# Layer 1's output projection as seven block products on two PSUM tiles

## The chip, the core and the metric

The kernel runs on one core of a Trainium2 chip. The metric is the device time of one execution in microseconds (us). The engines of a core work through their own instruction queues, each in order, and wait for each other by semaphores: TensorE (PE in the profile, its weight loads PEld), VectorE (DVE), ScalarE (ACT), GpSimd (POOL), and SyncE (SP), which here issues most of the DMAs.

## The reference

Two attention layers with group norm in front and a residual around each, on x of 128 rows x 256 positions x 256 channels, in float32. Layer 0 is row attention with a pair bias from z and a gate. Layer 1, where the change is, is banded attention:

```python
qkv = x2 @ w_in.T + b_in                 # x2 = group norm of x, (128, 256, 256)
q, k, v = heads of qkv                   # 4 heads of 64
scores = einsum('bhid,bhjd->bhij', q, k) / sqrt(64)
scores = where(|i - j| <= 16, scores, -inf)
out = einsum('bhij,bhjd->bhid', softmax(scores), v)
y = out @ w_out.T + b_out
x = x + y
```

The last product, `out @ w_out.T`, is the output projection.

## The kernel before

Layer 1 handles the 128 rows in 64 pairs (`NP`); class `Pair1` holds one pair, and its two rows are numbered `r` = 0 and 1. Channels lie on the partitions in two blocks (`KC` = 2) of 128; positions are cut in two blocks (`NB` = 2) of 128.

The order of all instructions is written out by hand: under `tc.manual_schedule()` every engine gets its instructions in the order in which the Python code makes them. The loop `for p in range(NP - 1)` (line 2169) has five pairs in hand: `was` (p - 1) is finished, `now` (p) has its scores and its first row applied, `nxt` (p + 1) has q, k and v computed, `nn` (p + 2) is normalised, and `n3` (p + 3) is loaded and transposed. One iteration has, in order:

- `now.scores(0)`, `now.scores(1)`: scores of both rows on PE (L2013), exponentials on ACT (L2022), the band's mask multiplied in by POOL (L2024).
- `was.apply(1)`: exponentials times v, and the sums of the exponentials, for row 1 (L2038, L2046). Even and odd key blocks go to two accumulators each. ACT copies the odd one (`copy_sums` L2057, `copy_odd` L2060), DVE adds the even one (`join_sums` L2063, `join_odd` L2066), `invert` takes the reciprocal (L2069), and `weigh` multiplies the two into `oT` (L2074), from SBUF to SBUF.
- Between these stand `nxt.product(n, i)` and `nxt.join(n, i)` for q (n = 0) and k (n = 1), and later for v (n = 2). q, k and v are made of 2 x 2 blocks each; seven block products in place of eight suffice, with sums of weight blocks (`wst`, made once by `mix_weights`) and of input blocks (`dT`, made by `differences` on POOL, L1922 to L1925). Products 1, 6, 7, 4 run up one accumulator x: after each, ACT copies what stands there (to `u`, or as an output block), before the next product is added on it. Products 2, 5, 3 use a second accumulator y, and after each a `join` on DVE adds y and a copy in `u` to give an output block. q and k use tiles of 256 columns (L1960), v uses two halves of 128 (L1956). x and y are whole PSUM tiles of tags `s0` and `s1`, shared with the scores; q and v use `s0`, k uses `s1`.
- `was.out_row(0)`, and further down `was.out_block(1, 0)` and `was.out_block(1, 1)`: the output projection. A row takes two blocks of positions, and a block takes two products of 256 columns (L2092). `keep_row` adds the residual `xt` on DVE (L2100), and after row 1 SP writes the pair out (L2108).
- `nn.centre(k)`: normalisation on ACT (L1909). `nn.add_bias()`: the residual plus the output bias on POOL (L1915). `n3.turn()`: transposition on DVE (L1904). `some_checks`: comparisons on DVE from a queue of checks, two an iteration until the queue is empty, more in the last eight pairs.

In this order the two blocks of `was.out_row(0)` stand between products 7 and 4 of q and k, `was.join_odd(1)` stands after the joins 5, and `nn.centre(1)`, `nn.differences()`, `nn.add_bias()` and `n3.turn()` are at the end of the iteration.

[...]Four are the tags `s0` and `s1`, two hold `o_eo`, the even and odd outputs of `apply`. The last two are one tile `su_y` of shape `[P, 2, 2, I]`: its first half of each bank (`su_eo`) takes the sums of even and odd blocks, its second halves together take the projection of a row (`self.y`).

SP issues in the order of the code too: the loads of a pair (`xs` in four DMAs and `xt`) when `Pair1` is made, at the start of an iteration, then the sums of `weigh` (L2079), then the output.

Of the kernel before, what the change touches and what calls it, by code (L numbers as in the profile page):

```python
# [773 lines left out]
def fast_kernel(  # L774
# [134 lines left out]
    def rows(ap, s0, n):  # L909
        return ap[s0 : s0 + n].rearrange("s (b p) c -> p (s b) c", p=P)  # L910
# [914 lines left out]
    with tc.tile_pool(name="l1", bufs=2) as sb, tc.tile_pool(  # L1825
# [10 lines left out]
        dev = lrs[0][:, :G]  # L1836
        each = head.rearrange("p n d -> p (n d)").rearrange("p (n c) -> p n c", n=2)
        wst = sb.tile([P, 4, 3, P], F32, name="wst", bufs=1)

        def norm1():  # L1840

# [20 lines left out]
        def mix_weights():  # L1862

            a = [[w_in[:, k].rearrange("p (n m c) -> p m n c", n=3, m=KC)[:, m] for k in range(KC)]
                 for m in range(KC)]
            s1, s2, s3, s4 = (wst[:, n] for n in range(4))
            nc.gpsimd.tensor_tensor(s1, a[1][0], a[1][1], ALU.add)
            nc.gpsimd.tensor_tensor(s2, s1, a[0][0], ALU.subtract)
            nc.gpsimd.tensor_tensor(s3, a[0][0], a[1][0], ALU.subtract)
            nc.gpsimd.tensor_tensor(s4, a[0][1], s2, ALU.subtract)  # L1870


        o_eo = [ps_o.tile([P, 2, I], F32, name=f"ps_o1_{n}", tag=f"o{n}") for n in range(2)]
        su_y = ps_o.tile([P, 2, 2, I], F32, name="ps_su_y1", tag="su")
        su_eo = [su_y[:, n, 0] for n in range(2)]
        for n in range(2):
            nc.vector.memset(o_eo[n], 0.0)
        nc.vector.memset(su_y, 0.0)

        class Pair1:  # L1880

# [54 lines left out]
            def product(self, n, i):  # L1936

                if len(self.ps) == n:
                    self.ps.append([mm1("ps_qk", n % 2) for _ in range(2)])
                    self.u.append(sm.tile([P, 3, I], F32, name="u1", tag=f"u{n}", bufs=2))  # L1940
                x, y = (ps[:, :I] for ps in self.ps[n])
                w = lambda m, k: w_in[:, k, n * C + m * P : n * C + (m + 1) * P]
                b = lambda k, r: self.xgT[:, k, r * I : (r + 1) * I]
                to, lhs, rhs, start = {
                    1: (x, w(0, 0), b(0, 0), True),
                    2: (y, w(0, 1), b(1, 0), True),
                    6: (x, wst[:, 1, n], self.dT[:, 1], False),
                    5: (y, wst[:, 0, n], self.dT[:, 0], True),
                    7: (x, wst[:, 2, n], self.dT[:, 2], False),
                    4: (x, w(1, 1), self.dT[:, 3], False),  # L1950
                    3: (y, wst[:, 3, n], b(1, 1), False),
                }[i]
                if n == 2:
                    for b in range(NB):
                        at = slice(b * P, (b + 1) * P)
                        nc.tensor.matmul(  # L1956
                            to[:, at], rhs[:, at], lhs, start=start and b == 0, stop=True, skip_group_check=True
                        )
                else:
                    nc.tensor.matmul(to, lhs, rhs, start=start, stop=True, skip_group_check=True)  # L1960
                u = self.u[n]
                if i in (2, 5, 3):
                    return
                at = (1, 6, 7, 4).index(i)
                to = self.to[n](1, 0) if i == 4 else u[:, at]
                if n == 2:
                    nc.scalar.copy(to, x.rearrange("p (b c) -> p b c", b=NB) if i == 4 else x)
                else:
                    nc.scalar.activation(to, x, AF.Identity, bias=bin_c[:, n * KC + (at > 1) : n * KC + (at > 1) + 1])  # L1969
# [59 lines left out]
            def apply(self, r):  # L2029


                e = self.es[r]
                gap = q0(2) - q0(0)
                for a in range(2):
                    for j in range(NK // 2):
                        for h in range(H1):
                            for k in (2 * j, 2 * j + 1):
                                nc.tensor.matmul(  # L2038
                                    o_eo[k % 2][h * DH : (h + 1) * DH, a, q0(k) : q0(k) + W],
                                    self.v[half(k), r, j, h * D1 + a * DH : h * D1 + (a + 1) * DH],  # L2040
                                    e[half(k), h % 2, h // 2, j * W : (j + 1) * W], start=True, stop=True,
                                )
                for h in range(H1):
                    for n in range(2):
                        two = su_y[h * DH : (h + 1) * DH, n].rearrange("p a i -> p (a i)")
                        nc.tensor.matmul(  # L2046
                            two[:, q0(n) : q0(n) + 2 * gap].rearrange("p (j w) -> p j w", w=gap)[:, :, :W],
                            ones[half(n), :DH],
                            e[half(n), h % 2, h // 2, :].rearrange("p (j w) -> p j w", w=W), start=True, stop=True,
                        )  # L2050
# [34 lines left out]

            def out_block(self, r, b):
                if b == 0:
                    self.y = su_y[:, :, 1]
                    if self.p == NP - 1:
                        self.y = mm1("ps_y1", r).rearrange("p (b c) -> p b c", b=NB)  # L2090
                for k in range(KC):
                    nc.tensor.matmul(  # L2092
                        self.y[:, b], self.oT[r][:, k, b * P : (b + 1) * P], w_out[:, k, :],
                        start=(k == 0), stop=(k == KC - 1),
                    )

            def keep_row(self, r):
                if r == 0:
                    self.yo = sb.tile([P, 2 * NB, C], F32, name="yo", tag="yo")
                nc.vector.tensor_tensor(  # L2100
                    self.yo[:, r * NB : (r + 1) * NB, :], self.y,
                    self.xt[:, r * NB : (r + 1) * NB, :], ALU.add,
                )
                s0 = 2 * self.p
                if self.p == NP - 1:
                    nc.sync.dma_start(rows(out, s0 + r, 1), self.yo[:, r * NB : (r + 1) * NB, :])
                elif r == 1:
                    nc.sync.dma_start(rows(out, s0, 2), self.yo)  # L2108
# [39 lines left out]
        with tc.manual_schedule():  # L2148
# [16 lines left out]
            look_all(eb.rearrange("p h b i -> p (h b i)"), math.exp(-20.0))  # L2165
            n_eb = cols[0]

            was = Nobody()
            for p in range(NP - 1):
                nn = pair1(p + 2) if p == 0 else n3  # L2170
                n3 = pair1(p + 3)
# [10 lines left out]

                now.scores(0)
                now.scores(1)
                was.apply(1)
                nxt.begin_fast()
                was.copy_sums(1)
# [1 line left out]
                was.copy_odd(1)  # L2189
                nxt.product(1, 1)  # L2190
                was.join_sums(1)
                for n in range(2):
                    nxt.product(n, 2)
                    nxt.join(n, 2)
                was.invert(1)
                some_checks(p > 0)
                for i in (6, 5, 7):
                    for n in range(2):
                        nxt.product(n, i)
                for n in range(2):  # L2200
                    nxt.join(n, 5)
                was.join_odd(1)
                was.weigh(1)
                was.out_row(0)
                for n in range(2):
                    nxt.product(n, 4)
                    nxt.product(n, 3)
                    nxt.join(n, 3)
                fast = p < NP - 2
                if fast:  # L2210
                    nxt.product(2, 1)
                    nxt.product(2, 2)
                    nxt.join(2, 2)
                nn.centre(0)
                some_checks(2 if p > NP - LATE else 0)

                now.apply(0)
                now.copy_sums(0)
                if fast:
                    nxt.product(2, 6)  # L2220
                    nxt.product(2, 5)
                now.copy_odd(0)
                now.join_sums(0)
                was.out_block(1, 0)
                if fast:
                    nxt.product(2, 7)
                now.join_odd(0)
                some_checks(2 if p > NP - LATE else p > 0)
                was.out_block(1, 1)
                if fast:  # L2230
                    nxt.join(2, 5)
                was.keep_row(1)
                if fast:
                    nxt.product(2, 4)
                    nxt.product(2, 3)
                    nxt.join(2, 3)
                now.invert(0)
                now.weigh(0)
                nn.centre(1)
                nn.differences()  # L2240
                nn.add_bias()
                n3.turn()
                if p == NP // 2:
                    below(0, n_eb, math.exp(20.0))
                    below(n_eb, n_mask, 1e15)
                was, now, nxt = now, nxt, nn

            now.scores(0)
            was.apply(1)
            was.copy_sums(1)  # L2250
            was.copy_odd(1)
# [102 lines left out]
```

## Time and profile before

| what | value |
|---|---|
| median of three timed runs | 3128.2 us (3127.22 to 3128.6) |
| profiled execution, its own time | 3127.13 us |
| its span, first to last instruction | 3125.4 us |
| mean granted TensorE clock | 0.986 |
| layer 1 begins, about | 2000 us after the span's start |
| mean of one L2092 record (projection), 128x256 | 385 ns |
| mean of one L1956 record (v), 128x128 | 283 ns |
| mean of L2024 (mask on POOL), 128x384 | 1001 ns |
| mean of L2069 (reciprocal on DVE), 128x256 | 1743 ns |

Matmuls are pipelined, so a record's own duration is longer than the time it adds; the chain that ended last shows what each group adds. Each float32 matmul of the program has two records. "Idle before" with a releaser in square brackets says how long an engine had been idle and what it waited for. The durations of POOL are rougher than those of the others.

### The profile page before, as it was taken

To read this page: it belongs to the slowest core of one execution; us is meant where nothing else is said; L and a number is where in the kernel's file an instruction comes from. 1 tells how busy PE (TensorE), PEld (TensorE's weight loads), DVE (VectorE), ACT (ScalarE), POOL (GpSimd) and SP (SyncE) were. 2 spreads that over 40 slices of the span, in tenths; PEclk is the share of its full clock that TensorE was granted. 3 is DMA by queue.
4 is the path that set the end of the run, shared out by engine and by line. 5 is a ranking of instruction groups with operands and counts; after the bars stand their busy time and mean duration, and the time that the engine had idled before them with its cause. 6 is when DMAs were issued, how large, how long until landed. Compare 5 with 4: busy or idle time off the path is not lost.

```text
span 3125.4 us, 80592 instructions
## 1 busy us (share of the span) xinstructions
PE 3014.3 (96%) x33638; PEld 2097.3 (67%) x33638; DVE 2398.2 (77%) x4008; ACT 1575.7 (50%) x2639; POOL 2268.6 (73%) x1633
## 2 busy tenths in 40 slices
PE   5689999999999999999999999899999999999998
PEld 4355555566555556555555655688888888888886
DVE  7986677777777777777777777688878777777788
ACT  3454444444444444444444444355555555555553
POOL 3469899888889989888898987455555555555553
PEclk9799999999999999999999999999999999999999
DMA  9952433433333332333343332543434344444441
GB/s 359 390 180 52 99 72 97 99 68 91 91 99 71 98 99 68 91 91 99 70 98 99 64 94 68 118 97 90 97 90 96 91 96 91 95 92 93 94 95 50
DMA packets 690774, 327.90 MB, mean 105 GB/s; under 512 B 538624, under 2 KB 639872, under 8 KB 689248
## 3 DMA queue, kind: packets, MB, share of 16 engines
q1 hardware_dynamic: 686000, 320.02, 40.5%
q8 instruction: 266, 4.36, 0.6%
q10 hardware_dynamic: 4400, 2.63, 0.3%
q14 instruction: 108, 0.88, 0.1%
HBM read 253.83 MB, written 68.74 MB: 103 GB/s over the span
## 4 chain that ended last, share of the span: by engine, by line
PE 92%; DMA 4%; DVE 2%; POOL 1%; ACT 1%; issue 0%; SPq 0%; ACTq 0%; POOLq 0%; DVEq 0%
PE ps_p L1364 21%; PE ps_qk L1960 13%; PE ps_sc L1401 9%; PE ps_ov L1436 8%; PE ps_su_y L2092 7%; PE ps_y L1491 7%; PE ps_qk L1956 7%; PE ps_v L1382 7%; PE ps_o L2038 4%; PE ps_su L1444 3%; PE ps_sc L2013 3%; PE ps_su_y L2046 2%; DMA zt<-in_z_dram 2%; DMA xa<-in_x_dram 1%; PE ps_t L1143 1%; DVE st L1199 1%
## 5 line engine op out<-in xcount | busy, mean ns | idle before, releaser
L1425 POOL TENSOR_TENSOR eboth<-e 128x512 f32<-128x512 f32 x512 | 743.9, 1474 | 176.9 <-PE ps_su L1444 97.7
L1421 DVE TENSOR_TENSOR e<-ps_sc,eb 128x1024 f32<-128x1024 f32 x384 | 458.4, 1222 | 292.8 <-ACT ps_sc L1413 292.7
L1413 ACT ACTIVATE ps_sc<-ps_sc 128x1024 f32<-128x1024 f32 x384 | 375.5, 1007 | 438.7 <-PE ps_sc L1401 313.0
L1401 PE MATMUL ps_sc<-qT,kT 32*128 32x256 f32 x4096 | 294.8, 401 | 0.0
L1923 POOL TENSOR_TENSOR dT<-xgT,dT 128x256 f32<-128x256 f32 x63 | 46.1, 731 | 314.3 <-ACT xgT L1909 314.3
L2024 POOL TENSOR_TENSOR e<-e,bw 128x384 f32<-128x384 f32 x256 | 248.4, 1001 | 10.8 <-ACT e L2022 10.8
L2092 PE MATMUL ps_su_y<-w_out,oT 128*128 128x256 f32 x1008 | 254.5, 385 | 0.9 <-DVE sums L2063 0.9
L1401 PEld LDWEIGHTS ps_sc<-qT,kT 32*128 32x128 f32 x4096 | 185.9, 184 | 102.0 <-issue 91.4
L1491 PEld LDWEIGHTS ps_y<-wo,oT 128*128 128x128 f32 x1024 | 194.3, 190 | 87.6 <-issue 44.3
L1491 PE MATMUL ps_y<-wo,oT 128*128 128x256 f32 x1024 | 243.0, 380 | 6.6 <-POOL oT L1481 5.8
L1364 PE MATMUL ps_p<-xnT,wq 128*128 128x512 f32 x512 | 247.5, 605 | 0.1
L1436 PE MATMUL ps_ov<-e,v 128*32 128x256 f32 x4096 | 247.6, 382 | 0.0
L1364 PE MATMUL ps_p<-xgT,wg 128*128 128x512 f32 x512 | 247.3, 605 | 0.0
L1382 PE MATMUL ps_v<-wv,xnT 128*128 128x256 f32 x1024 | 241.8, 379 | 0.0
L1364 PE MATMUL ps_p<-xnT,wk 128*128 128x512 f32 x512 | 240.7, 592 | 0.0
L1382 PEld LDWEIGHTS ps_v<-wv,xnT 128*128 128x128 f32 x1024 | 194.5, 190 | 54.0 <-issue 30.9
L2069 DVE RECIPROCAL rv<-sums 128x256 f32<-128x256 f32 x128 | 223.1, 1743 | 0.1
L1969 ACT ACTIVATE u<-ps_qk,bin_c 128x256 f32<-128x256 f32 x378 | 174.9, 477 | 94.6 <-PE ps_qk L1960 94.6
L2092 PEld LDWEIGHTS ps_su_y<-w_out,oT 128*128 128x128 f32 x1008 | 181.8, 190 | 22.4 <-DVE sums L2063 1.3
L1436 PEld LDWEIGHTS ps_ov<-e,v 128*32 128x32 f32 x4096 | 120.0, 109 | 108.5 <-issue 41.8
L1364 PEld LDWEIGHTS ps_p<-xnT,wk 128*128 128x128 f32 x512 | 97.2, 190 | 122.8 <-issue 122.6
L1922 POOL TENSOR_TENSOR dT<-xgT 128x256 f32<-128x256 f32 x63 | 46.0, 730 | 183.2 <-ACT xgT L1909 183.2
(229 smaller groups left out, 6602.6 us busy)
## 6 DMA issues: line engine op xcount, KB each, us to landing
xa<-in_x_dram SPq DMA_DIRECT2D x8, 4096.0 KB
xt<-in_x_dram SPq DMA_DIRECT2D x64, 512.0 KB
x<-xo SPq DMA_DIRECT2D x16, 2048.0 KB
xt<-x SPq DMA_DIRECT2D x64, 512.0 KB
rvb<-rsum SPq DMA_DIRECT2D x252, 128.0 KB
xs<-x SPq DMA_DIRECT2D x252, 128.0 KB
out_dram<-yo SPq DMA_DIRECT2D x63, 512.0 KB
xs<-in_x_dram SPq DMA_DIRECT2D x248, 128.0 KB
```

What stands on the lines that cost most here:

```text
L1364: nc.tensor.matmul(ps, w[:, k, m * P : (m + 1) * P], getattr(self, src)[:, k, :], start=(k == 0), stop=(k == KC - 1),)
L1382: nc.tensor.matmul(self.ps_v[:, b * C : (b + 1) * C], self.xnT[:, k, t * P : (t + 1) * P], wv[:, k, :], start=(k == 0), stop=(k == KC - 1),)
L1401: nc.tensor.matmul(self.pss[q // 2][:, q % 2, b, :], self.kT[rs, c, r * I + b * P : r * I + (b + 1) * P], self.qT[rs, c, r * I : (r + 1) * I],
L1413: nc.scalar.activation(self.pss[a], ps, AF.Exp)
L1421: nc.vector.tensor_tensor(es[a], pss[a], eb[:, h : h + 2], ALU.mult)
L1425: nc.gpsimd.tensor_tensor(t, es[a][:, :, 0, :], es[a][:, :, 1, :], ALU.add)
L1436: nc.tensor.matmul(ov[q * D0 : (q + 1) * D0, c, :], self.v[:, r, b, h * D0 : (h + 1) * D0], es[q // 2][:, q % 2, b, :], start=(b == 0), st ...
L1491: nc.tensor.matmul(self.ps_y[:, b * C : (b + 1) * C], self.oT[r][:, k, b * P : (b + 1) * P], wo[:, k, :], start=(k == 0), stop=(k == KC - 1),)
L1960: nc.tensor.matmul(to, lhs, rhs, start=start, stop=True, skip_group_check=True)
L2024: nc.gpsimd.tensor_tensor(e[:, q], e[:, q], bcast(bw.rearrange("p b w -> p (b w)"), 1, KC), ALU.mult)
L2069: nc.vector.reciprocal(self.rv[:, r, :], self.sums)
L2092: nc.tensor.matmul(self.y[:, b], self.oT[r][:, k, b * P : (b + 1) * P], w_out[:, k, :], start=(k == 0), stop=(k == KC - 1),)
```

## The change

The output projection of a pair takes the form that q, k and v have already. `mix_weights` also makes four sums of blocks of `w_out` (`wso`). A new `row_sums` makes four sums of blocks of the pair's two `oT` on POOL (`oS`, 128x256 each). `out_product(i)` multiplies, in two halves of 128 positions by 128 columns; ACT copies after products 1, 6, 7 (to `uy`) and 4 (to the output tile `yo`), and `out_join(i)` on DVE makes the other three blocks. The residual is added for the whole pair in one instruction by `keep_rows` on POOL, an iteration later (`old`), which also issues the output DMA. Only the last two pairs differ: pairs NP - 2 and NP - 1 keep `out_row` or `out_block` and `keep_row`, which for pair NP - 2 takes two instructions a row.

`su_y` becomes two tiles of one bank each. Each holds one of the two sums in its first half and one accumulator of the projection in its second: x beside the even sums, y beside the odd.

In the loop several steps are moved: `was.join_odd(1)` ahead of the products 2; product 3 of k from behind product 3 of q to the end of the iteration; `nn.centre(1)`, `nn.differences()`, `nn.add_bias()` and `n3.turn()` from the end to before `now.apply(0)`; `now.join_sums(0)` ahead of `now.copy_odd(0)`. The copies `u` of q, k and v have one buffer in place of two.

```diff
+        wso = sb.tile([P, 4, P], F32, name="wso", bufs=1)
...
+            a = [[w_out[:, k, m * P : (m + 1) * P] for k in range(KC)] for m in range(KC)]
+            s1, s2, s3, s4 = (wso[:, n] for n in range(4))
+            nc.gpsimd.tensor_tensor(s1, a[1][0], a[1][1], ALU.add)
+            nc.gpsimd.tensor_tensor(s2, s1, a[0][0], ALU.subtract)
+            nc.gpsimd.tensor_tensor(s3, a[0][0], a[1][0], ALU.subtract)
+            nc.gpsimd.tensor_tensor(s4, a[0][1], s2, ALU.subtract)
...
-        su_y = ps_o.tile([P, 2, 2, I], F32, name="ps_su_y1", tag="su")
-        su_eo = [su_y[:, n, 0] for n in range(2)]
+        su_y = [ps_o.tile([P, 2, I], F32, name=f"ps_su_y{n}", tag=f"su{n}") for n in range(2)]
+        su_eo = [t[:, 0] for t in su_y]
...
-                    self.u.append(sm.tile([P, 3, I], F32, name="u1", tag=f"u{n}", bufs=2))
+                    self.u.append(sm.tile([P, 3, I], F32, name="u1", tag=f"u{n}", bufs=1))
...
+            def row_sums(self):
+                self.oS = sb.tile([P, 4, I], F32, name="oS1", tag="oS", bufs=1)
+                b = [[self.oT[r][:, k, :] for r in range(2)] for k in range(KC)]
+                t1, t2, t3, t4 = (self.oS[:, n] for n in range(4))
+                nc.gpsimd.tensor_tensor(t1, b[0][1], b[0][0], ALU.subtract)
+                nc.gpsimd.tensor_tensor(t2, b[1][1], t1, ALU.subtract)
+                nc.gpsimd.tensor_tensor(t3, b[1][1], b[0][1], ALU.subtract)
+                nc.gpsimd.tensor_tensor(t4, b[1][0], t2, ALU.subtract)
...
+            def out_product(self, i):
+                if i == 1:
+                    self.yo = sb.tile([P, 2 * NB, C], F32, name="yo", tag="yo")
+                    self.uy = sm.tile([P, 3, I], F32, name="uy1", tag="uy", bufs=1)
+                x, y = (t[:, 1] for t in su_y)
+                w = lambda m, k: w_out[:, k, m * P : (m + 1) * P]
+                b = lambda k, r: self.oT[r][:, k, :]
+                to, rhs, lhs, start = {
+                    1: (x, w(0, 0), b(0, 0), True),
+                    2: (y, w(0, 1), b(1, 0), True),
+                    6: (x, wso[:, 1], self.oS[:, 1], False),
+                    5: (y, wso[:, 0], self.oS[:, 0], True),
+                    7: (x, wso[:, 2], self.oS[:, 2], False),
+                    4: (x, w(1, 1), self.oS[:, 3], False),
+                    3: (y, wso[:, 3], b(1, 1), False),
+                }[i]
+                for n in range(NB):
+                    at = slice(n * P, (n + 1) * P)
+                    nc.tensor.matmul(
+                        to[:, at], lhs[:, at], rhs, start=start and n == 0, stop=True, skip_group_check=True
+                    )
+                if i in (2, 5, 3):
+                    return
+                if i == 4:
+                    nc.scalar.copy(self.quarter(1, 0), x.rearrange("p (b c) -> p b c", b=NB))
+                else:
+                    nc.scalar.copy(self.uy[:, (1, 6, 7).index(i)], x)
+
+            def out_join(self, i):
+                m, r, at = {2: (0, 0, 0), 5: (1, 1, 2), 3: (0, 1, 1)}[i]
+                y, u = (t.rearrange("p (b c) -> p b c", b=NB) for t in (su_y[1][:, 1], self.uy[:, at]))
+                nc.vector.tensor_tensor(self.quarter(m, r), y, u, ALU.add)
+
+            def keep_rows(self):
+                nc.gpsimd.tensor_tensor(self.yo, self.yo, self.xt, ALU.add)
+                nc.sync.dma_start(rows(out, 2 * self.p, 2), self.yo)
```

And the loop:

```diff
                 now.scores(0)
                 now.scores(1)
+                old.keep_rows()
                 was.apply(1)
...
                 was.join_sums(1)
+                was.join_odd(1)
                 for n in range(2):
                     nxt.product(n, 2)
                     nxt.join(n, 2)
                 was.invert(1)
-                some_checks(p > 0)
                 for i in (6, 5, 7):
...
                     nxt.join(n, 5)
-                was.join_odd(1)
+                some_checks(0 if p > NP - LATE else p > 0)
+                nxt.product(0, 4)
+                nxt.product(1, 4)
+                nxt.product(0, 3)
+                nxt.join(0, 3)
                 was.weigh(1)
-                was.out_row(0)
-                for n in range(2):
-                    nxt.product(n, 4)
-                    nxt.product(n, 3)
-                    nxt.join(n, 3)
+                nn.add_bias()
+                was.row_sums()
                 fast = p < NP - 2
                 if fast:
                     nxt.product(2, 1)
                     nxt.product(2, 2)
                     nxt.join(2, 2)
                 nn.centre(0)
-                some_checks(2 if p > NP - LATE else 0)
+                nn.centre(1)
+                nn.differences()
+                n3.turn()
 
                 now.apply(0)
                 now.copy_sums(0)
                 if fast:
                     nxt.product(2, 6)
                     nxt.product(2, 5)
+                now.join_sums(0)
+                was.out_product(1)
+                was.out_product(2)
+                was.out_join(2)
                 now.copy_odd(0)
-                now.join_sums(0)
-                was.out_block(1, 0)
+                now.join_odd(0)
                 if fast:
                     nxt.product(2, 7)
-                now.join_odd(0)
-                some_checks(2 if p > NP - LATE else p > 0)
-                was.out_block(1, 1)
-                if fast:
                     nxt.join(2, 5)
-                was.keep_row(1)
+                was.out_product(6)
+                was.out_product(5)
                 if fast:
                     nxt.product(2, 4)
+                some_checks(2 if p > NP - LATE else p > 0)
+                was.out_product(7)
+                was.out_join(5)
+                nxt.product(1, 3)
+                nxt.join(1, 3)
+                if fast:
                     nxt.product(2, 3)
                     nxt.join(2, 3)
+                was.out_product(4)
+                was.out_product(3)
+                was.out_join(3)
                 now.invert(0)
                 now.weigh(0)
-                nn.centre(1)
-                nn.differences()
-                nn.add_bias()
-                n3.turn()
+                some_checks(2 if p > NP - LATE else 0)
...
-                was, now, nxt = now, nxt, nn
+                old, was, now, nxt = was, now, nxt, nn
```

After the loop, `old.keep_rows()` is called once more behind `now.scores(0)`.

More of the change, by code (lines that the diff above doesn't have):

```diff
@@ L1870, in mix_weights @@
             nc.gpsimd.tensor_tensor(s4, a[0][1], s2, ALU.subtract)
+            a = [[w_out[:, k, m * P : (m + 1) * P] for k in range(KC)] for m in range(KC)]
[4 more added lines that the diff above has]
+            nc.gpsimd.tensor_tensor(s4, a[0][1], s2, ALU.subtract)
         o_eo = [ps_o.tile([P, 2, I], F32, name=f"ps_o1_{n}", tag=f"o{n}") for n in range(2)]
-        su_y = ps_o.tile([P, 2, 2, I], F32, name="ps_su_y1", tag="su")
-        su_eo = [su_y[:, n, 0] for n in range(2)]
+        su_y = [ps_o.tile([P, 2, I], F32, name=f"ps_su_y{n}", tag=f"su{n}") for n in range(2)]
+        su_eo = [t[:, 0] for t in su_y]
         for n in range(2):
             nc.vector.memset(o_eo[n], 0.0)
-        nc.vector.memset(su_y, 0.0)
+            nc.vector.memset(su_y[n], 0.0)
         class Pair1:
@@ L2044, in apply @@
                     for n in range(2):
-                        two = su_y[h * DH : (h + 1) * DH, n].rearrange("p a i -> p (a i)")
+                        two = su_y[n][h * DH : (h + 1) * DH].rearrange("p a i -> p (a i)")
                         nc.tensor.matmul(
@@ L2087, in out_block @@
                 if b == 0:
-                    self.y = su_y[:, :, 1]
+                    self.y = [t[:, 1] for t in su_y]
                     if self.p == NP - 1:
-                        self.y = mm1("ps_y1", r).rearrange("p (b c) -> p b c", b=NB)
+                        ps = mm1("ps_y1", r)
+                        self.y = [ps[:, n * C : (n + 1) * C] for n in range(NB)]
+                        self.whole = ps
                 for k in range(KC):
                     nc.tensor.matmul(
-                        self.y[:, b], self.oT[r][:, k, b * P : (b + 1) * P], w_out[:, k, :],
+                        self.y[b], self.oT[r][:, k, b * P : (b + 1) * P], w_out[:, k, :],
@@ new lines, in quarter @@
+            def quarter(self, m, r):
+                return self.yo[:, r * NB : (r + 1) * NB, m * P : (m + 1) * P]
+            def out_product(self, i):
[25 more added lines that the diff above has]
+                    nc.scalar.copy(self.uy[:, (1, 6, 7).index(i)], x)
@@ L2099, in keep_row @@
                     self.yo = sb.tile([P, 2 * NB, C], F32, name="yo", tag="yo")
[L2100 to L2103, printed above, removed]
+                if self.p == NP - 1:
+                    nc.vector.tensor_tensor(
+                        self.yo[:, r * NB : (r + 1) * NB, :], self.whole.rearrange("p (b c) -> p b c", b=NB),
+                        self.xt[:, r * NB : (r + 1) * NB, :], ALU.add,
+                    )
+                for t in range(r * NB, (r + 1) * NB if self.p < NP - 1 else 0):
+                    nc.vector.tensor_tensor(self.yo[:, t, :], self.y[t - r * NB], self.xt[:, t, :], ALU.add)
                 s0 = 2 * self.p
@@ L2166, in fast_kernel @@
             n_eb = cols[0]
-            was = Nobody()
+            old = was = Nobody()
             for p in range(NP - 1):
@@ L2245, in fast_kernel @@
                     below(n_eb, n_mask, 1e15)
-                was, now, nxt = now, nxt, nn
+                old, was, now, nxt = was, now, nxt, nn
             now.scores(0)
+            old.keep_rows()
             was.apply(1)
```

## The prediction

> **What bounds the kernel now.** First the page: busy time of the engines and the chain that ended last.
>
> ```profile
> PE 3014.3 (96%) x33638; PEld 2097.3 (67%) x33638; DVE 2398.2 (77%) x4008; ACT 1575.7 (50%) x2639; POOL 2268.6 (73%) x1633
> ...
> PE 92%; DMA 4%; DVE 2%; POOL 1%; ACT 1%; issue 0%; SPq 0%; ACTq 0%; POOLq 0%; DVEq 0%
> ```
>
> TensorE (PE) is the chain. The change is inside layer 1, so next a stretch of layer 1 in the view by windows (busy us of each engine):
>
> ```profile
> core 0: us, PE busy (x) PEld busy (x) DVE busy (x) ACT busy (x) POOL busy (x), PEclk, DMA share, GB/s
> 2500.00:2800.00 300.00, 298.95 (x5076) 259.06 (x5078) 230.60 (x347) 169.51 (x378) 161.55 (x153) 1.00 0.42 92
> ```
>
> PE is full, VectorE (DVE) at 77%, GpSimd (POOL) at 54%. Then the chain of waits in order of time, over one iteration of the pair loop (start, length, what):
>
> ```profile
> 2537.77 1.48 PE ps_sc L2013 x64
> ...
> 2540.54 4.51 PE ps_qk L1960 x20
> 2545.05 1.73 PE ps_su_y L2092 x8
> 2546.78 1.73 PE ps_qk L1960 x8
> 2548.51 1.11 PE ps_qk L1956 x8
> ...
> 2550.90 1.09 PE ps_qk L1956 x8
> 2551.99 0.96 PE ps_su_y L2092 x4
> 2552.95 0.45 PE ps_qk L1956 x4
> 2553.40 0.86 PE ps_su_y L2092 x4
> 2554.26 0.89 PE ps_qk L1956 x8
> ```
>
> The next iteration starts at 2555.16: 17.38 us each. L2092 is the projection; every product is two records. A record of 256 columns takes 0.216 us (1.73/8), one of 128 columns 0.111 (0.89/8). Two pieces are longer than that: 1.11 (0.22 of stall) and 0.96 (0.09).
>
> In this schedule the projection does a second job: it fills PE while ScalarE (ACT) and DVE answer. The first iteration has no pair to project, and shows what the place looks like without it, in the same view:
>
> ```profile
> 2002.98 4.17 PE ps_qk L1960 x18
> 2007.14 0.02 issue
> 2007.17 0.48 ACT u L1969
> 2007.65 0.14 issue
> 2007.79 1.97 PE ps_qk L1960 x8
> ```
>
> Product 7 of q ends at 2007.14, ACT copies it, and product 4 of q starts effectively at 2009.76 - 1.73 = 2008.03: 0.89 us, of which product 7 of k fills 0.43. PE loses 0.46.
>
> **What the Trainium skill says.** "SBUF — State Buffer", section "Who interferes with whom": a DVE instruction with two SBUF inputs contends with a GpSimd instruction that reads SBUF, and the first to issue has the shared pair for the whole instruction while the other blocks. The timeline agrees, for `weigh` (L2074, 0.69 us when free):
>
> ```profile
> 3064.22 0.73 POOL L1925 TENSOR_TENSOR dT<-xgT,dT 128x256 f32<-128x256 f32 x1
> 3064.26 1.24 DVE L2074 TENSOR_TENSOR oT<-odd,rv 128x512 f32<-128x512 f32 x1
> 3064.90 2.83 POOL L1915 TENSOR_TENSOR xt<-xt,bout_r 128x1024 f32<-128x1024 f32 x1
> ```
>
> `weigh` came 0.04 after a POOL instruction, waited until it ended and then took the boundary: POOL's next one shows 2.83 instead of 2.36. So a waiting `weigh` costs POOL 0.5, and costs DVE the rest of POOL's instruction.
>
> "PSUM — Partial Sum Buffer", section "PSUM bank collisions raise a hardware error": two engines are to be kept apart by bank, not by address. The trace agrees that the projection, writing other columns, waits for the reading of the sums:
>
> ```profile
> 2551.35 0.42 DVE L2063 TENSOR_TENSOR sums<-ps_su_y,sums 128x256 f32<-128x256 f32 x1 [1.20 <-ACT sums L2057]
> ```
>
> It ends at 2551.77; the first projection block starts effectively at 2552.95 - 4 x 0.216 = 2552.08, 0.31 later. From ACT it is 2007.65 to 2008.03, 0.38. I use 0.32 for a release of PE by ACT or DVE, and 0.04 from PE's end to ACT or DVE (2007.14 to 2007.17).
>
> **The change part by part.** Times in an iteration count from its first score.
>
> *PE work.* Out go 16 records of 0.216 = 3.46; in come 7 products in 2 halves, 28 records of 0.111 = 3.11. Gain 0.35 an iteration.
>
> *Join of the odd heads, moved ahead of the joins of product 2.* It needs ACT's copy, which now ends at 4.39 (2541.58 + 0.58 - 2537.77). 4.43 + 0.61 = 5.04 for q's join, which ends 5.46; product 5 of q may start at 5.79. PE would be there at 5.55 (start 2.96, six products of 0.43). Stall 0.24; before, that join ended at 4.79 and there was none.
>
> *Row 0's projection taken out from between products 7 and 4.* The stall of the first iteration, 0.46, now comes every time.
>
> *Product 3 of k moved to the end.* After product 3 of q only the first value product (0.44) precedes the second, which needs q's last join (its PSUM tile): 0.04 + 0.42 + 0.32 = 0.78. Stall 0.34, of which 0.22 is there already.
>
> So far PE reaches: product 7 of k 7.52, product 4 of q 7.98, product 3 of q done 9.28, value products done 10.5, `apply` of the row 11.8, value products 6 and 5 done 12.9 (1.09, as in the chain). The first projection product waits for `join_sums`: copy of the sums 11.83 to 12.2, join to 12.66, release 12.98. That is 0.1, as before. From there eleven products follow (ten of 0.44, one of 0.43): 4.85, end 17.83. In this tail I checked each ACT and DVE answer (copy to next product on the same accumulator 0.04 + 0.37 + 0.32 = 0.73, cover 0.88; the last, ACT copy and join before product 3, 1.19 with cover 1.31): hidden, by as little as 0.1.
>
> *POOL.* It gets `row_sums`, four of 0.70, and `keep_rows`, 128x1024, which I price as L1915 of that size: 2.36, spacing 2.33. Sum with the old 9.6: about 14.8 of 17 to 18 us. Its order from the exponentials on: four masks `e` (L2024, 3.86) from 1.49, `keep_rows`, `add_bias`, then `row_sums`. In before it did the masks late, after `add_bias`, and had 5.1 and 2.8 us of idle time; now differences and sums end near 16.6, before the next masks. `weigh(0)` of the previous iteration arrives near 2.2 (out join 0.05 to 0.47, reciprocal 1.74), inside the masks, and puts POOL back by 0.5. So `keep_rows` starts at 5.85, `add_bias` at 8.2 and ends at 10.53.
>
> *`weigh(1)`* comes on DVE after q's last join, ready at 9.65, inside `add_bias`: locked out until 10.53, its follower may start at 11.05. Behind it in DVE's queue: join of the values to 11.4, `turn`, now moved from the end of the iteration to here, and `join_sums` (`turn` start to that join's end 1.55, as 2540.54 to 2542.09). It ends at 12.93, not 12.66, and the projection starts at 13.25; end at 18.1. Bounds for this lock: nothing, if `weigh(1)` meets a boundary (17.83), to a whole `add_bias` met at its start (+1). I take 18.06, with 0.68 lost per iteration.
>
> *DVE* loses two `keep_row` of 0.68 and gets three joins of 0.42. *ACT* gets four copies of 0.37 (12.3 us in all); moving `centre(1)` ahead of the sums' copy fits, since v's copy ends at 10.1 and the two centres at 11.6, before 11.83. *Queues:* on SP the output DMA now waits for `keep_rows` near 8.2 and the loads of the next pairs stand behind it and behind the sums' DMA: some 5 us of issue, then landing (at the loop's start 3.7 us from the last issue, 1993.4, to the `turn` it released, 1997.1) by about the start of the iteration that turns them at 11.3; hidden. Buffers of `u` halved: last read by q's, k's and v's joins a half iteration before they are rewritten; nothing. Four sums of weights before the loop: 128x128 on POOL, under 1 us each, inside its 4.33 of idle time at 1995.42; nothing. Two memsets for one: nothing.
>
> *Sum.* 61 iterations with both a pair to project and values: 61 x 0.68 = 41.5. The first gets 0.2, the last loop iteration, with no value products to fill between the projection's, about 1.5. 3127.1 (profiled execution, span 3125.4) + 43 = 3170; the three timed runs have 3128.2 as median, 1 us above, which I leave out.
>
> **Rivals.**
> 1. Stalls only, 0.20: the lock does not bind, because `weigh(1)` slips in between two POOL instructions or its delay is absorbed. 61 x 0.45 + 2 = 29: 3156. For it: only 0.3 us separate the two cases; against: POOL runs without a pause from 1.49 to 10.5.
> 2. Faster, 0.12: the three stalls are absorbed, by the weight loads being issued ahead or an order on ACT and DVE I misread, and the 0.35 stands: 3127 - 61 x 0.35 = 3106. It decides as soon as the stalls together stay under 0.35. Against: the 0.46 alone, measured on the same instructions, cancels it.
> 3. A cancel to within 0.2%, 0.05: about 3128.
> 4. More, 0.11: a second place in the tight tail binds, above all product 3 behind the fifth join, or a check (its scalar comparison also can be locked out) in front of it. 0.4 to 0.5 more an iteration: 3199.
>
> **Numbers.** The forecast has 0.52. Time 3170. Range 3140 to 3200: it takes in rival 1 and most of 4, and leaves out the faster case and no change. 0.2%, some 6 us, is what a measurement of this kernel can tell: faster 0.12, same 0.05, slower 0.83.
>
> **What would show it.** An iteration of 18.1 (17.8 for rival 1, 17.0 for rival 2). In the chain of waits, ACT `u` ahead of product 4 and DVE `sums` ahead of the first projection product, in every iteration; PE's busy share in layer 1 down to some 94%. `weigh(1)` at 1.3 us or more, ending with `add_bias`, and POOL above 80%. Wrong if PE's chain is unbroken, if `weigh(1)` shows 0.69, or if the join of the odd heads ends before 5.0.

## The result and the profile after

The changed kernel takes 3168.6 us in the median of four runs (3167.7 to 3170.1), the kernel before 3127.7 in the runs beside it. The ratio is 1.0133, with a 95% interval of 1.0121 to 1.0144: slower, as forecast, and 1.4 us from the forecast of 3170.

The page of the changed kernel, busy time and the chain that ended last:

```profile
PE 3034.7 (96%) x34382; PEld 2089.7 (66%) x34382; DVE 2391.4 (76%) x4073; ACT 1664.3 (53%) x2887; POOL 2586.8 (82%) x1947
...
PE 88%; DMA 4%; DVE 4%; POOL 2%; ACT 1%; issue 1%; SPq 0%; ACTq 0%; POOLq 0%; DVEq 0%
```

The span grew by 40.5 us (3165.9 against 3125.4), and PE's share of the chain that ended last fell from 92% to 88%. POOL is busy for 318 us more. The stretch of layer 1 shown of before, in the view by windows:

```profile
2500.00:2800.00 300.00, 294.84 (x5120) 248.46 (x5119) 219.36 (x352) 187.70 (x432) 242.32 (x233) 1.00 0.38 89
```

PE shows 98% busy although it works less: a record's busy time also covers some of the time in which a product waits. In the chain below, for instance, six records of q and k take 1.55 us where 1.30 is their usual time. POOL went from 54% to 81%. Where PE's time went, the chain of waits of one iteration says (start, length, what):

```profile
2538.61 1.48 PE ps_sc L2020 x64
...
2541.37 4.30 PE ps_qk L1967 x18
2545.68 0.02 issue
2545.70 0.48 ACT u L1976
2546.18 0.14 issue
2546.32 1.55 PE ps_qk L1967 x6
2547.86 0.02 issue
2547.89 0.44 DVE qT L1983
2548.32 0.04 issue
2548.37 0.71 PE ps_qk L1963 x4
...
2550.36 1.09 PE ps_qk L1963 x8
2551.45 1.10 PE ps_su_y L2138 x8
```

The reader is to see three stalls that the chain of before does not have in this form. The first 18 records of q and k take 4.30 us; of before it was 4.51 for 20, so 4.08 for 18: 0.22 lost. Then ACT's copy `u` stands alone in the chain: from the end of product 7 of q to the effective start of product 4 (2547.87 less six records, 1.30) are 0.89 us, of which product 7 of k fills 0.43. Then a join on DVE: 2547.86 to 2548.64, of which the first value product fills 0.44. The next iteration starts at 2556.56, after 17.95 us; 17.38 before.

### The profile page after: what moved, and what is told of

The parts are those of the page before. It is cut to its first block, busy times and chain, and to the rows that moved or that the text cites. A ratio compares the mean times of both kernels' runs of the same rounds, so it can differ in the third digit from the quotient of the medians.

```text
span 3165.9 us, 82989 instructions
## 1 busy us (share of the span) xinstructions
PE 3034.7 (96%) x34382; PEld 2089.7 (66%) x34382; DVE 2391.4 (76%) x4073; ACT 1664.3 (53%) x2887; POOL 2586.8 (82%) x1947
## 4 chain that ended last, share of the span: by engine, by line
PE 88%; DMA 4%; DVE 4%; POOL 2%; ACT 1%; issue 1%; SPq 0%; ACTq 0%; POOLq 0%; DVEq 0%
PE ps_p L1364 21%; PE ps_qk L1967 12%; PE ps_sc L1401 9%; PE ps_ov L1436 7%; PE ps_y L1491 7%; PE ps_v L1382 7%; PE ps_su_y L2138 6%; PE ps_qk L1963 6%; PE ps_su L1444 3%; PE ps_o L2045 3%; PE ps_sc L2020 3%; DMA zt<-in_z_dram 2%; PE ps_su_y L2053 2%; DMA xa<-in_x_dram 1%; DVE qT L1983 1%
## 5 line engine op out<-in xcount | busy, mean ns | idle before, releaser
L2031 POOL TENSOR_TENSOR e<-e,bw 128x384 f32<-128x384 f32 x256 | 276.9, 1111 | 166.7 <-ACT e L2029 166.7
L1436 PEld LDWEIGHTS ps_ov<-e,v 128*32 128x32 f32 x4096 | 120.0, 109 | 108.2 <-issue 41.5
L2151 DVE TENSOR_TENSOR yo<-ps_su_y,uy 128x256 f32<-128x256 f32 x186 | 79.0, 425 | 146.5 <-ACT uy L2146 105.0
L1967 PE MATMUL ps_qk<-dT,wst 128*128 128x256 f32 x756 | 186.5, 388 | 0.9 <-DVE qT L1983 0.9
L1116 POOL TENSOR_TENSOR zrs<-zrs,mhalf 128x32 f32<-128x32 f32 (+1 forms) x19 | 88.0, 4636 | 115.1 <-DVE zrs L1109 115.1
L1371 ACT ACTIVATE gT<-ps_p,bg_c 128x512 f32<-128x512 f32 x128 | 88.0, 687 | 175.0 <-PE ps_p L1364 175.0
```

The source lines that it names most:

```text
L1436: nc.tensor.matmul(ov[q * D0 : (q + 1) * D0, c, :], self.v[:, r, b, h * D0 : (h + 1) * D0], es[q // 2][:, q % 2, b, :], start=(b == 0), st ...
L2031: nc.gpsimd.tensor_tensor(e[:, q], e[:, q], bcast(bw.rearrange("p b w -> p (b w)"), 1, KC), ALU.mult)
```

## The experiments

Two measures serve throughout. The length of an iteration is taken from the starts of `turn` (the transposition on DVE) in the profiled execution: "common" is the most frequent length, "mean" is over 55 iterations from the fifth on. Lengths are in us. Time and ratio come from the timed runs, beside runs of the kernel before on the same chip.

| kernel | common us | mean us | time us | ratio to before (95%) |
|---|---|---|---|---|
| before | 17.38 | 17.46 | 3127.7 | 1 |
| changed | 17.96 | 18.04 | 3168.6 | 1.0133 (1.0121 to 1.0144) |
| e1_order | 17.97 | 17.98 | 3164.6 | 1.0117 (1.0100 to 1.0134) |
| e2_bias | 17.85 | 18.03 | 3169.4 | 1.0134 (1.0117 to 1.0151) |
| e3_both | 17.20 | 17.39 | 3129.3 | 1.0008 (0.9999 to 1.0016) |
| e4_gap | 17.41 | 17.59 | 3142.7 | 1.0052 (1.0035 to 1.0069) |
| e5_odd | 17.64 | 17.89 | 3155.7 | 1.0089 (1.0072 to 1.0106) |
| e6_three | 17.51 | 17.66 | 3148.0 | 1.0073 (1.0057 to 1.0088) |
| e7_odd_late | 17.24, then 16.92 | 17.25 | 3119.6 | 0.9976 (0.9965 to 0.9986) |
| e8_loads | as e7_odd_late | 17.46 | 3134.7 | 1.0024 (1.0014 to 1.0035) |
| e9_before_shift | 17.38 | 17.45 | 3126.5 | 0.9996 (0.9987 to 1.0005) |
| e10_checks | 16.92 | 17.14 | 3113.8 | 0.9959 (0.9946 to 0.9973) |
| e11_uncovered | 17.63 | 17.71 | 3143.8 | 1.0055 (1.0039 to 1.0070) |
| e12_no_xs | 16.92 | 17.08 | 3111.9 | 0.9952 (0.9937 to 0.9967) |

**The theories.** Mine, formed after the result: in the changed kernel two chains of nearly equal length end at the first projection product. One is PE's own, with its three stalls. The other runs from the exponentials over POOL's masks, `keep_rows` and `add_bias` to `weigh(1)` on DVE, which starts while POOL's `add_bias` runs and does not end before it, and on over `turn` and `join_sums`. Rivals: the stalls are all, and the second chain is of no consequence; or the seven products in halves are too dear themselves.

**The order alone.** All three stalls are taken out by order, POOL is left as it is.

```diff
-                was.join_odd(1)
                 for n in range(2):
                     nxt.product(n, 2)
                     nxt.join(n, 2)
                 was.invert(1)
-                for i in (6, 5, 7):
-                    for n in range(2):
-                        nxt.product(n, i)
+                was.join_odd(1)
+                for n, i in ((0, 6), (1, 6), (0, 5), (0, 7), (1, 7), (1, 5)):
+                    nxt.product(n, i)
...
                 nxt.product(0, 4)
-                nxt.product(1, 4)
                 nxt.product(0, 3)
                 nxt.join(0, 3)
+                nxt.product(1, 4)
```

> Changed kernel with the three stalls of the q and k products taken out by order alone: the join of the odd heads behind the reciprocal, product 5 of k behind both products 7, product 3 of q ahead of product 4 of k. Two chains (mine): the chain POOL masks, keep_rows, add_bias, weigh(1), turn, join_sums still releases the projection 13.05 us after the scores, so the iteration stays at 17.9 to 17.96 us and the time at 3165 to 3169. Stalls alone: 0.24 + 0.47 + 0.33 go, iteration 16.9, time 3105. The seven-product form itself too dear: no gain here either, but then none in e3_both.

The iteration takes 17.97, so nothing was gained. The timeline of e1_order says why. By POOL's masks its iteration starts at 2538.74, 0.13 later than the one shown of the changed kernel:

```profile
2546.79 2.37 POOL L1922 TENSOR_TENSOR xt<-xt,bout_r 128x1024 f32<-128x1024 f32 x1
...
2547.63 2.08 DVE L2081 TENSOR_TENSOR oT<-odd,rv 128x512 f32<-128x512 f32 x1
2549.63 0.41 DVE L1983 TENSOR_TENSOR v<-ps_qk,u 128x256 f32<-128x256 f32 x1
2549.97 1.23 DVE L1911 STREAM_TRANSPOSE xT<-xs 128x1024 f32<-128x1024 f32 x1
2551.12 0.38 DVE L2070 TENSOR_TENSOR sums<-ps_su_y,sums 128x256 f32<-128x256 f32 x1
```

`weigh` (L2081) comes 0.73 earlier in the iteration than in the changed kernel (8.89 against 9.62) and is held that much longer: 2.08 us, until POOL's `add_bias` (L1922) has ended. `join_sums` ends 12.76 us into the iteration, and 12.73 in the changed kernel. One us of stalls was taken from PE, and the projection starts when it did.

**POOL's order alone.**

```diff
                 was.weigh(1)
-                nn.add_bias()
                 was.row_sums()
...
                 nn.differences()
+                nn.add_bias()
```

> Changed kernel with add_bias put behind the differences on POOL, so that weigh(1) meets no POOL instruction. Two chains: the projection is then held by the copy and join of the sums behind apply, 0.07 to 0.1 us earlier than now: iteration 17.87, time 3162 to 3165. Stalls alone: nothing, 3168. If the lock were the whole loss: 0.5 an iteration, 3138.

The common iteration is 17.85, as expected, and `weigh(1)` takes 0.68. But the time did not fall: 26 of the 55 iterations are over 0.05 longer than the common one, 17 in the changed kernel, and the mean stays at 18.03.

**Both edits.**

> Both edits, e1_order and e2_bias. Two chains: only now the three stalls count, 1.0 to 1.07 us an iteration, iteration 16.9 to 17.0, time 3103 to 3110, under the kernel before. Stalls alone: the same as e1_order. Seven-product form itself too dear: above 3150.

Together they bring 39 us where each alone brought 4 or nothing. It is a miss all the same: the iteration takes 17.20 and not 16.9. Its chain of waits has this place:

```profile
2540.78 5.01 PE ps_qk L1967 x22
2545.78 0.04 issue
2545.82 1.13 PE ps_qk L1967 x4
```

Four records take 1.13 instead of 0.86: product 3 of q waits for its join 5. My edit had put the join of the odd heads in front of that join on DVE. In e7_odd_late it stands behind the joins 5, as in the kernel before:

> e3_both with the join of the odd heads behind the joins 5, where the kernel before has it. e3_both's typical iteration was 17.20 and not 16.9 because product 3 of q waited 0.3 us for its join 5, which stood behind the join of the odd heads on VectorE: 16.9 now, 18 us less than e3_both, 3111. If something else holds that product: 3129.

The iteration takes 16.92 from about the 27th on, with 26 records of q and k in one unbroken piece of 5.87. The earlier iterations, as long as there are checks to do, stay at 17.24 for the most part, so that the time is 3119.6 and not 3111. The kernel is faster than the one before, by 0.24%.

**The three stalls one by one**, each on top of e2_bias: product 5 of k behind both products 7 (e4_gap), the join of the odd heads behind the joins 2 (e5_odd), product 3 of q ahead of product 4 of k (e6_three).

> e2_bias and of the order only product 5 of k behind both products 7, which covers the wait between product 7 and product 4 of q. Two chains: 0.46 less than e2_bias, iteration 17.42, time 3134 to 3139. If that wait isn't worth its 0.46 (as other waits take its place): as e2_bias, 3163.

> e2_bias and of the order only the join of the odd heads moved back behind the joins 2 and the reciprocal. Two chains: 0.24 less than e2_bias's typical 17.85, so 17.61 us an iteration and about 15 us less in time than e2_bias, 3154. If this wait is not worth its size: 3169.

> e2_bias and of the order only product 3 of q ahead of product 4 of k, so that product 4 of k and the first value product cover the join before the second value product. Two chains: 0.33 less than e2_bias's typical 17.85, so 17.52 us, 3148 to 3152. If the wait moves to product 3 itself: as e2_bias, 3169.

From the common 17.85 each took 0.44, 0.21 and 0.34. The times came out 27, 14 and 21 us under e2_bias, close to 62 iterations of these, e4_gap a little above its expected range.

**The cover, in the kernel before.** Only this is moved; nothing else of the change is in it:

```diff
                 was.weigh(1)
-                was.out_row(0)
                 for n in range(2):
                     nxt.product(n, 4)
                     nxt.product(n, 3)
                     nxt.join(n, 3)
+                was.out_row(0)
```

> Kernel before with one move: row 0's projection from between products 7 and 4 to behind the products 3 of q and k. Nothing else of the change. Projection as cover (mine): 0.46 of wait opens between product 7 of k and product 4 of q, and the 0.22 before the second value product closes: typical iteration 17.62 instead of 17.38, 3140 to 3143. If the cover is of no consequence: 17.16 to 17.38, 3114 to 3127.

The iteration takes 17.63, one hundredth from the forecast. Its chain of waits shows the gap that the projection had filled:

```profile
2552.94 0.02 issue
2552.96 0.48 ACT u L1969
2553.45 0.14 issue
2553.58 1.97 PE ps_qk L1960 x8
```

**The irregular iterations.** In the changed kernel and its variants more iterations run longer than the common one. In the chain they appear as "issue" among the short instructions of `apply`, as here in e2_bias:

```profile
2560.33 0.28 PE ps_su_y L2053 x5
2560.61 0.25 issue
2560.86 0.53 PE ps_su_y L2053 x9
```

One theory is that they come from the loads: these now leave SP in the middle of an iteration, and their traffic is where it was not before. Two tests move the loads: back to the start of the iteration in e8_loads, and to the middle in the kernel before.

> e7_odd_late with the loads of a pair made one iteration earlier and keep_rows at the end of an iteration, so that the output DMA and the loads behind it leave at the start of an iteration, as in the kernel before, and not at its middle. If the loads' traffic delays TensorE's instructions where many short ones stand (scores and apply): the irregular longer iterations go, mean near the typical 16.9, 3098 to 3103. If they don't come from the loads: as e7_odd_late within 3 us.

> Kernel before, whose only change is that a pair's output DMA is issued one iteration later behind weigh(1), so that the loads behind it on SP leave in the middle of an iteration, as in the changed kernel. If the loads' place makes irregular long iterations: typical 17.38 stays, the mean rises by 0.1 to 0.2, 3133 to 3140. If not: 3127.

Both contradict it. e8_loads got longer by 15 us, with some waits for issue of up to 1.9 us. Its edit also moves `keep_rows` on POOL and makes the loads an iteration earlier, so these 15 us have no single cause. The kernel before did not change: 0.9996, with an interval that holds 1. A third test leaves the loads of `xs` out of e10_checks: the DMA engines' busy share in 2200 to 2800 us falls from 0.42 to 0.21.

> e10_checks which loads the blocks to be transposed (xs) only for pairs 1 to 3 and transposes those again for all later pairs, so that the loads of xs for pairs 4 to 63 are left out. If the traffic of these small packets delays TensorE's instructions and makes the irregular long iterations: all at the typical 16.92, 3095 to 3102. If they come from elsewhere: as e10_checks within 4 us.

The mean falls by 0.06 of the 0.22 that it stands over the common length, and the time by less than 2 us. So the loads of `xs` are not the main cause.

The kept traces narrow it down. Count a wait where the `apply` that follows the scores ends more than 0.05 us later than usual, over the iterations of the loop with p from 1 to 57. The iterations 3, 10, 17 and so on, every seventh up to 52, have one in the changed kernel and in all ten of its variants, e8_loads and e12_no_xs included. The traces also list the DMA packets of a queue that the profile calls "instruction", two or three of 16 KB an iteration. In e10_checks such a packet of 16 KB starts between 0.5 us before and 0.9 us after the start of 22 iterations, and 21 of these 22 have a wait; of the other 35 only one has. In e12_no_xs it is 20 of 22 and one of 35, and in the kernel before, which has fewer waits, 9 of 11 and one of 46. The supply of instructions is therefore the nearest suspect. The band of 1.4 us is fitted to these traces and no run moves those packets on their own, so this is not shown as the cause.

**The check.** e10_checks puts the first check of an iteration at its end:

```diff
-                some_checks(0 if p > NP - LATE else p > 0)
...
                 now.weigh(0)
-                some_checks(2 if p > NP - LATE else 0)
+                some_checks(2 if p > NP - LATE else p > 0)
```

> e7_odd_late with the first check of an iteration moved from ahead of join 3 of q to the end of the iteration. In the first 25 iterations e7_odd_late had 17.24 us, in the rest 16.92, and the check delays the join before the second value product: 16.92 to 16.95 in all now, 6 to 8 us less than e7_odd_late, 3112. If the checks' iterations are long for another reason: 3119.

The iterations of 17.24 are gone, and the time is 3113.8, or 0.9959 of the kernel before: the fastest version that makes all its loads. The common iteration is 0.46 shorter than before, the mean one only 0.32, because of the irregular iterations.

No run gives the kernel before the same care in its order. Its chain still has stalls of 0.22 and 0.09 an iteration, so how much of the 0.4% is due to the seven products and how much to order is not separated.

## Why the prediction was right, point by point

- *PE's work, 0.35 less.* The chain of e10_checks over most of an iteration:

```profile
2534.47 5.87 PE ps_qk L1967 x26
...
2543.62 0.99 PE ps_su_y L2138 x8
2544.61 0.45 PE ps_qk L1963 x4
2545.06 0.89 PE ps_su_y L2138 x8
2545.95 0.45 PE ps_qk L1963 x4
2546.40 0.45 PE ps_su_y L2138 x4
2546.84 0.43 PE ps_qk L1967 x2
2547.28 0.44 PE ps_qk L1963 x4
2547.72 0.89 PE ps_su_y L2138 x8
```

  The four pieces of projection (L2138) take 0.99 + 0.89 + 0.45 + 0.89 = 3.22; before they took 1.73 + 0.96 + 0.86 = 3.55. The gain is 0.33, and the halves are no dearer than v's (0.89 for eight records in both). In the changed kernel the gain was there and lost elsewhere.
- *The three stalls.* Forecast 0.24, 0.46, 0.34 (0.22 of the last present before). In the changed kernel's chain 0.22, 0.46, 0.34; taken out one by one 0.21, 0.44, 0.34. The first iteration of the kernel before had shown the largest of them to the hundredth, and e11_uncovered reproduced it there.
- *The lock.* `weigh(1)` came at 9.62 (forecast 9.65) and took 1.31 us, until `add_bias` ended. Here a size was off: "locked out until 10.53", with the follower at 11.05. The timeline of the changed kernel:

```profile
2546.64 2.35 POOL L1922 TENSOR_TENSOR xt<-xt,bout_r 128x1024 f32<-128x1024 f32 x1
...
2548.23 1.31 DVE L2081 TENSOR_TENSOR oT<-odd,rv 128x512 f32<-128x512 f32 x1
2549.47 0.41 DVE L1983 TENSOR_TENSOR v<-ps_qk,u 128x256 f32<-128x256 f32 x1
```

  From 2538.61, `add_bias` ends at 10.38 and the follower starts at 10.86: POOL reached it 0.15 sooner, having begun its masks 0.05 earlier and lost less to the first `weigh`. The first projection product then starts effectively at 2552.55 - 0.89 = 2551.66, at 13.05 and not 13.25. So the lock, DVE held until POOL's instruction ends, cost 0.11 of the common iteration (e2_bias), and not 0.23, and the iteration is 17.96, not 18.06. (The working of the prediction itself ends at 18.1; it took 18.06 without giving a reason.) The parts add up: 17.38 - 0.33 + 0.22 + 0.46 + 0.12 + 0.11 = 17.96, where 0.12 is the third stall less the part that was there before.
- *The iteration's sum.* 61 x 0.58 = 35.4 where I had 41.5. From the first exponentials to those of the last loop iteration the two profiles differ by 36.9.
- *The ends.* I had 1.7 for the first and the last iteration. From the last loop iteration's exponentials to the end the profiles differ by 4.7 (49.3 against 44.6), and the loop began 1.0 earlier. In the last iteration, with no value products in between, the projection also waits for `row_sums`, which I had not counted. So 36.9 + 4.7 - 1.0 = 40.5, against the forecast 43: two sizes were off in opposite senses, and the agreement with 3170 is in part luck. The irregular iterations are luck too: the prediction did not know of them, and they cancel only because they put 0.08 on the mean iteration in both kernels (17.46 over 17.38, 18.04 over 17.96). In e2_bias they put on 0.18.
- *The tail.* The answers of ACT and DVE behind the first projection product are hidden in the common iteration: its pieces are 0.45, 0.89, 0.45, 0.45, 0.43, 0.44, 0.89 without a gap. The loads are hidden too; no `turn` waits for a DMA in 2100 to 3000.
- *What I said would show it.* ACT `u` in the chain, `weigh(1)` at 1.3 and POOL above 80% came. DVE `sums` did not come into the chain of the iteration shown, though PE's first piece of projection takes 1.10 and not 0.89: it starts effectively 0.32 after that join ends, so these 0.21 are put down to that wait. PE's busy share is 98% and not 94%: busy time of matmul records did not show stalls of 1 us in 18.
- *Rival 1* had the stalls without the lock at 17.83 and 3156. e2_bias is that case: 17.85, but 3169, as its iterations were more often irregular.

## What to carry to other kernels

Before a block of work is moved or made shorter, look at what its time covers. Here the 1.73 us of row 0's projection also hid the answer of ACT after product 7 of q, and taking it out of that place opened a stall of 0.46, more than the 0.33 that the shorter projection saves. Two other moves in the order opened 0.34 more. Where a change leaves two chains of nearly equal length, mending either alone can show nothing, so test the mends together before giving one up. And order can outweigh the number of instructions: the same seven products, with five moves in the order, go from 1.3% slower to 0.4% faster.

## What the runs showed of the hardware that had not been expected

- What a DVE instruction with both inputs in SBUF loses beside POOL depends on when it comes. `weigh(1)` takes 0.68 where it meets no POOL instruction (e2_bias), 1.31 in the changed kernel, and 2.08 in e1_order, where it starts 0.84 after the start of a POOL instruction of 2.37 and ends 0.55 after its end.
- How many waits for issue there are and how much they cost are two things. In e1_order, where PE waits for DVE later in the iteration anyway, 23 of 57 iterations have such a wait, but only 4 of 55 are over 0.05 longer than the common one. Where PE's own chain sets the end (e2_bias to e6_three, e10_checks) 25 to 31 of 55 are. The kernel before, also bound by PE, has only 10, as it has fewer waits.
